# Two AdaLN transformer layers: key and value products over two steps, in-place sums, and reordered heads and FFN ends

## The chip, the cores and the metric

The kernel runs on one core of a Trainium2 chip. The metric is the time of one execution on the device in microseconds (us), as the median of repeated runs; lower is better. A profile of one execution says where that time goes.

## The reference

Two transformer layers with adaptive layer norms on x of 4 x 512 x 512 (float32). Each layer computes six modulation rows per batch from a condition vector, then an attention block and an FFN block, each on a modulated layer norm of x and added back through a gate. The change lies in layer 1 alone, which is:

```python
h = layernorm(x) * (1 + ca) + sa
q = (h @ w_q).reshape(B, S, 8, 4, 128)     # 8 kv heads, 4 query heads each
k = (h @ w_k).reshape(B, S, 8, 128)
v = (h @ w_v).reshape(B, S, 8, 128)
scores = einsum('bqhgd,bkhd->bhgqk', q, k) * 128 ** -0.5, causal
attn = einsum('bhgqk,bkhd->bqhgd', softmax(scores), v)
x = x + ga * (attn.reshape(B, S, 4096) @ w_o)
h = layernorm(x) * (1 + cb) + sb
gate, up = h @ (gate_wq * gate_scale).T, h @ (up_wq * up_scale).T   # 1792 wide, int weights
x = x + gb * ((silu(gate) * up) @ (down_wq * down_scale).T)
```

Layer 0 (a small attention inside each token and an FFN with cluster masks) is untouched.

## The kernel before

**Order.** Until the FFN of layer 1 every engine runs its instructions in the order in which the program text issues them: layer 0 follows a list of step names, layer 1's attention the loop described here. Only layer 1's FFN is left to the scheduler of the framework. Transfers are issued by SP, one queue, in program order; an issue that has to wait holds up those behind it.

**Products in seven.** Each projection of layer 1 (q, k, v and the output o) is a 2 x 2 block product by seven smaller products with sums of blocks ahead of and behind it. `seven` makes seven *pieces*, each a group of matmuls into one PSUM bank and a call of `take`, which adds the bank into the result. Sums of the weights' blocks (`left_sums`, `right_sums`, by `sums_in` and `sums_wo`) run on POOL, in place in the weights' tile (tags wq, wk, wv, wo, one buffer each) and in a second tile (sq, sk, sv, so). For q, k and v, `gather` keeps running sums in two spare tiles `u` and writes the four quarters of the result. For o, seven running sums over the heads stand in `osum`.

**Heads and windows.** 4 batches x 8 kv heads make 32 heads n. A head has 4 query heads s, hence two pairs, and each pair is one step of the pipeline, `window(w)`: window 2n is the first of head n, window 2n+1 the second. Window w computes the scores of pair w+1 (8 tiles: 2 query heads x 4 row blocks of 512, 384, 256 and 128 columns) and the products with V of pair w. In between it runs a list of pieces, the *fill*, spread over 9 slots in order:

```python
share = [len(fill) // slots + (i < len(fill) % slots) for i in range(slots)]
```

In slot i the order is: `flip` of tile i-2 (a 32 x 32 block transpose on DVE), `divide` of tile i-1, `score` of tile i, the product with V (`value`) if i is 6 or 8 (the default of `values`), then that slot's fill. At the window's end `late` issues a load of weights, and `carry(w+1)` issues 16 transfers of 128 KB (SBUF to SBUF) that finish the transpose of the next pair's probabilities into one buffer, `turned`, which `value` reads. The flip of the last tile stands in DVE's order behind the evacuation of the fill of the last slot.

**What fills the windows.** Window 2n holds the seven q pieces of head n+1, and the seven k pieces (n odd, for heads n+1 and n+2) or v pieces (n even, for heads n and n+1). The order is `k[:5] + q[:5] + q[5:] + k[5:]` for odd n; for even n two v pieces alternate with one q piece, and q's last pieces come last. Its `late` is the load of q's weights for head n+2 (1 MB). Window 2n+1 holds the seven o pieces of head n-1, once per batch also four `turn_pieces` that transpose the next batch's norm; its `late` is the load of o's weights for head n (1 MB). The k or v load (0.5 MB) comes behind that window's `carry`. The list order of products is (1, 6, 2, 5, 3, 7, 4) for q, k and v, and (1, 2, 4, 7, 5, 6, 3) for o. Products 4 of q and 3 of o read a block of the loaded weights' tile itself, so the next load into it waits for them.

**The FFN** of layer 1 (`ffn_exact`): for each batch b and each of 14 blocks n of 128 hidden rows, `hidden` computes gate and up, the sigmoid and the two halves of the activation, and `down` adds the product of the block before into four PSUM banks; `leave` multiplies by the gate on DVE, adds to x on POOL and stores. `load` fetches int weights that POOL casts. `leave_attention` ends the attention's sums of batch 3 there.

Of the kernel before, what the change touches and what calls it, by code (L numbers as in the profile page):

```python
# [33 lines left out]
def adaln_two_layers(ctx: ExitStack, tc: tile.TileContext, a, out: bass.AP):  # L34
# [201 lines left out]
    def right_sums(engs, t, s, T1=None):  # L236

        B11, B12, B21, B22 = quarters(t)
        T3, T2, T4 = s[:, 0], s[:, 1], s[:, 2]
        T1 = B12 if T1 is None else T1  # L240
        engs[0].tensor_tensor(T3, B22, B12, SUB)
        engs[1].tensor_tensor(T1, B12, B11, SUB)
        engs[1].tensor_tensor(T2, B22, T1, SUB)  # L243
        engs[1].tensor_tensor(T4, T2, B21, SUB)
        return {1: B11, 2: B21, 3: B22, 4: T4, 5: T1, 6: T2, 7: T3}
# [8 lines left out]
    def sums_wo(n, place="o"):  # L254
        s = T["wp"].tile([P, 3, 2, HALF], F32, tag=f"s{place}", name="so")
        right["o", n] = right_sums((nc.gpsimd, nc.gpsimd), weights["o", n], s)

    def q3(ap):
# [463 lines left out]
    def bank(shape, name):  # L722
        return ps_sc.tile(shape, F32, tag="sc", name=name)
# [27 lines left out]
    def sums_h(b, engs):  # L751
        s = hp.tile([P, 4, 2, HALF], F32, tag="hT", name="hsum")
        right["h", b] = right_sums(engs, h1[b], s, s[:, 3])

# [4 lines left out]
    def gather(start, scale=None):  # L759

        u, c = {}, {}

        def plus(out, v, ps, sign=1):
            if scale is None:
                nc.vector.tensor_tensor(out, v, ps, ADD if sign > 0 else SUB)  # L765
            else:
                nc.vector.scalar_tensor_tensor(out, ps, sign * scale, v, ALU.mult, ADD)

        def take(i, ps):
            if i == 1:  # L770
                c[11], c[12], c[21], c[22] = start()
                size = ps.shape[1] * ps.shape[2]
                for j in (1, 2):
                    t = at.tile([P, size], F32, tag=f"u{j}_{size}", name=f"u{j}", bufs=1)
                    u[j] = t.rearrange("p (m n) -> p m n", m=ps.shape[1])
                if scale is None:
                    nc.scalar.copy(u[1], ps)
                else:
                    nc.scalar.mul(u[1], ps, scale)
            elif i == 6:  # L780
                plus(u[2], u[1], ps)
            elif i == 2:
                plus(c[11], u[1], ps)
            elif i == 5:
                plus(u[1], u[2], ps)
            elif i == 7:
                plus(c[22], u[1], ps)
                plus(u[2], u[2], ps)
            elif i == 3:
                plus(c[12], u[1], ps)  # L790
            else:
                plus(c[21], u[2], ps, -1)

        return take
# [23 lines left out]
    def v_pieces(m):  # L818

        def start():  # L820
            for n in (2 * m, 2 * m + 1):
                vs[n] = at.tile([P, NT, D1], F32, tag="v", name="v")
            v0, v1 = vs[2 * m], vs[2 * m + 1]
            return v0[:, :2], v0[:, 2:], v1[:, :2], v1[:, 2:]

        return seven(lambda: right["h", 2 * m // HKV], lambda: left["v", m], gather(start), SEVENTH)

    def o_pieces(n):
        def take(i, ps):
            if n % HKV == 0:  # L830
                nc.vector.tensor_copy(osum[:, i - 1], ps)
            else:
                nc.vector.tensor_tensor(osum[:, i - 1], osum[:, i - 1], ps, ADD)  # L833

        return seven(lambda: left["o", n], lambda: right["o", n], take, (1, 2, 4, 7, 5, 6, 3))

# [147 lines left out]
    def norm_pieces(xb):  # L984
# [24 lines left out]

        side = [lambda t=t: stats(t) for t in range(NT)]  # L1010
        return out_, side + [ve, nm] + [lambda t=t: xn(t) for t in range(NT)]

# [25 lines left out]
    def gates(pool):  # L1038

        dsb = pool.tile([P, E], F32, name="dsb")  # L1040
        nc.sync.dma_start(dsb, a["L1_ffn_down_scale"].partition_broadcast(P))
        for b in range(B):
            gb[b] = spread(1, 1, b, pool, f"gb{b}")
            nc.gpsimd.tensor_tensor(gb[b], gb[b], dsb, ALU.mult)
# [4 lines left out]
    def decide():  # L1049
        size = small.tile([P, 1], F32, tag="size", name="size", bufs=1)  # L1050
        nc.vector.tensor_reduce(size, sizes, AX.X, ALU.max)
        nc.vector.tensor_scalar(size, size, EXACT, None, ALU.is_gt)
        wide_ps = bank([P, 512], "wide_ps")
        nc.tensor.matmul(wide_ps[:1, :1], size, ones[:, 0:1], start=True, stop=True)
        nc.vector.tensor_copy(wide_i, wide_ps[:1, :1])
# [4 lines left out]
    def split_pieces(got):  # L1060

        def piece(c):
# [3 lines left out]
            for t in range(NT):  # L1066
                nc.tensor.transpose(
                    pt[:, t * P : (t + 1) * P], got["xn"][:, t, c * P : (c + 1) * P], ident
                )
            tm = at.tile([P, E], F32, tag=f"u{1 + c % 2}_{E}", name="tm", bufs=1)  # L1070
            nc.scalar.activation(
# [79 lines left out]
    load("v", 1)  # L1151
    pending = [("v", 1)]

    for n in range(NBLK):
# [5 lines left out]

        k = k_pieces(n // 2 + 1) if n % 2 and ahead else []
        v = v_pieces(n // 2) if n % 2 == 0 and n > 0 else []
        side, turns_ = [[], []], []
# [15 lines left out]
        if 0 < n <= len(pieces):  # L1179
            found = scan(n - 1)  # L1180
            side[1] += [lambda j=j: look(n - 1, j, found[j]) for j in range(2)]
        elif n == len(pieces) + 1:
            side[1].append(decide)
        elif n == len(pieces) + 2:
            side[1].append(small_loads)
        elif n == len(pieces) + 3:
            wide = nc.values_load(wide_i[0:1, 0:1], min_val=0, max_val=P)
        if n == 0:
            window(0, q[:5], values=(8, 9))
        elif ahead:  # L1190
            late = [lambda: load("q", n + 2)] if n + 2 < NBLK else []
            if n == 1:
                fill = q
            elif k:
                fill = k[:5] + q[:5] + q[5:] + k[5:]
            else:
                fill = [f for i in range(3) for f in (v[2 * i], v[2 * i + 1], q[i])] + v[6:] + q[3:]
            window(2 * n, fill, side[0], late)
        else:
            first_weights()  # L1200
            t = split_pieces(got)
            window(2 * n, o[:2] + t[:2] + o[2:3] + t[2:] + o[3:])

            last = o_pieces(n)
# [12 lines left out]
        if 0 < n < NBLK - 2:  # L1217
            sums_in("q", n + 2)
        while pending:
            sums_in(*pending.pop())  # L1220
        if n == 0:
            window(1, q[5:] + k_pieces(1), (), [lambda: load("q", 2)], (8, 9))
            sums_in("q", 2)
        else:
            window(2 * n + 1, o + turns_, side[1], [lambda: load("o", n)])
        sums_o(n)
        m = n // 2 + 2 if n else 2
        if (n % 2 and n > 1 or n == 0) and 2 * m < NBLK:
            load("k", m)
            pending.append(("k", m))  # L1230
        if n % 2 == 0 and n > 0 and n + 2 < NBLK:
            load("v", n // 2 + 1)
            pending.append(("v", n // 2 + 1))
        if behind:
# [4 lines left out]

    for b in (3, 1, 2, 0):  # L1240
        run(*get(b, x[b]))
# [5 lines left out]
    def ffn_exact():  # L1247
        with (
# [39 lines left out]
            def hidden(b, n):  # L1288
# [15 lines left out]
                nc.vector.scalar_tensor_tensor(sg, ps["up"], us, sg, ALU.mult, ALU.mult)  # L1304
                hi = fa.tile([P, S], F32R, tag="act_hi", name="act_hi")
                lo = fa.tile([P, S], F32R, tag="act_lo", name="act_lo")
                halves(hi, lo, sg)
                return hi, lo

            def down(b, n, act, acc):  # L1310
                f, c = divmod(n, NC_)
                w = gu0["down"] if b == f == 0 else gu["down", f]
                for t in range(NT):
                    for i in range(2):
# [4 lines left out]

            def leave(b, acc):  # L1320
                for t in range(NT):
                    tm = temp()
                    nc.vector.tensor_tensor(tm, acc[t], gb[b], ALU.mult)
                    nc.gpsimd.tensor_tensor(x[b][:, t, :], x[b][:, t, :], tm, ALU.add)
                    nc.sync.dma_start(out[b, t * P : (t + 1) * P, :], x[b][:, t, :])

            load(1)
            gates(fx)
            behind, rest = None, sum(leave_attention(B - 1, nc.vector, fx, "ga3", x[B - 1]), [])
            for b in range(B):  # L1330
                acc = [ps_acc.tile([P, 512], F32, tag="acc", name="acc") for t in range(NT)]
                for n in range(NI):
                    if b == 0 and n % NC_ == 0 and n // NC_ + 2 <= NB:
                        load((n // NC_ + 2) % NB)
                    act = hidden(b, n)
                    if behind is not None:
                        down(*behind)
                        if behind[1] == NI - 1:
                            leave(behind[0], behind[3])
                    behind = (b, n, act, acc)  # L1340
                    for _ in range(2):
                        if n > 0 and rest:
                            rest.pop(0)()
                    if n == (8 if b == 0 else 3) and b + 1 < B:
                        split_T(b + 1, normalized(b + 1, xn_place))
            down(*behind)
            leave(behind[0], behind[3])


# [88 lines left out]
```

## Time and profile before

| | us |
|---|---|
| median of 3 runs | 2109.91 (2109.38 to 2116.54) |
| profiled execution, its own time | 2109.82 |
| its span, first to last instruction | 2107.9 |
| PE busy | 2037.2 (97%) |
| DVE / ACT / POOL busy | 1360.0 / 873.5 / 748.6 |
| windows of layer 1's attention | from 211.6 to about 1766 |
| FFN of layer 1 | from 1780.7 to the end |

The page gives busy times per engine and the costliest groups of instructions; the list of waits says which engine waited for which releaser; the timeline of an engine gives each instruction's start and duration, and in square brackets the idle time before it. PE is TensorE, PEld its weight load, DVE VectorE, ACT ScalarE, POOL GpSimd, SPq the queue of SyncE that issues transfers. A float32 matmul stands in the trace as two instructions, and the printed durations of PE overlap: the distance between starts is what one costs.

### The profile page before, as it was taken

Reading aid. Unit: us, or ns where it says so; the run is one execution under the profiler, and the core shown is the slowest. Engines: PE = TensorE matmul, PEld = TensorE weight load, DVE = VectorE, ACT = ScalarE, POOL = GpSimd, SP = SyncE. Lnnn points to the kernel's source line nnn. Section 1 sums busy time; section 2 is a strip of 40 time slices with the busy share of each in tenths; the row PEclk is TensorE's granted clock in tenths of the full one; section 3 lists DMA queues with packets and bytes.
Section 4 is the critical chain, followed back from the end, with each engine's and each line's share of the span. In section 5 each row is a group of like instructions: output and inputs, shape, how many; then the busy total and the mean of one; then the engine's idle time right before and its main releaser. Section 6 shows DMA issues by size and latency. Waiting matters only on the chain.

```text
span 2107.9 us, 27434 instructions
## 1 busy us (share of the span) xinstructions
PE 2037.2 (97%) x9219; PEld 1582.1 (75%) x9219; DVE 1360.0 (65%) x3326; ACT 873.5 (41%) x1997; POOL 748.6 (36%) x653
## 2 busy tenths in 40 slices
PE   6999899999999999999999999999999998999998
PEld 4655677878787777778777777787777876788886
DVE  6766766666667666766676676666665665754543
ACT  3421544444444444544444444444444443332221
POOL 3315243334336343344463334436333422610010
PEclk8799999999999999999999999999999999999999
DMA  8311665665557666556665564656556555500000
GB/s 297 115 60 40 180 160 144 162 164 140 149 147 186 168 157 159 161 137 161 173 181 155 140 178 122 158 143 173 142 148 155 146 121 197 173 21 0 21 21 22
DMA packets 243624, 288.59 MB, mean 137 GB/s; under 512 B 23234, under 2 KB 184002, under 8 KB 243476
## 3 DMA queue, kind: packets, MB, share of 16 engines
q1 hardware_dynamic: 242948, 285.71, 50.1%
q8 instruction: 76, 1.25, 0.2%
q10 hardware_dynamic: 528, 1.05, 0.2%
q14 instruction: 72, 0.59, 0.1%
HBM read 142.99 MB, written 11.57 MB: 73 GB/s over the span
## 4 chain that ended last, share of the span: by engine, by line
PE 80%; DMA 7%; SPq 5%; DVE 3%; issue 2%; POOL 2%; ACT 1%; POOLq 0%; ACTq 0%; DVEq 0%
PE quarter L733 37%; PE av L917 13%; PE sc L868 9%; PE acc L1315 5%; SPq L908 5%; PE p_up L1296 4%; PE p_gate L1296 4%; DMA x<-x 4%; DMA wq<-in_L_attn_w_q_dram 2%; PE ffn L621 2%; PE lnT L464 1%; PE modps L377 1%; PE lg L580 1%; PE qkv_ps L494 1%; PE modT_ps L390 1%
## 5 line engine op out<-in xcount | busy, mean ns | idle before, releaser
L868 PE MATMUL sc<-kT,qT 128*128 128x512 f32 (+3 forms) x1024 | 359.9, 434 | 0.0
L917 PE MATMUL av<-x,v 128*128 128x512 f32 x1008 | 299.6, 441 | 28.9 <-DMA x<-x 13.9
L917 PEld LDWEIGHTS av<-x,v 128*128 128x128 f32 x1008 | 190.2, 193 | 143.4 <-issue 87.4
L883 ACT ACTIVATE x<-x,rden 128x512 f32<-128x512 f32 (+3 forms) x256 | 143.8, 562 | 359.6 <-DVE rden L882 359.5
L871 DVE TENSOR_REDUCE nmx<-sc 128x1 f32<-128x512 f32 (+3 forms) x512 | 251.3, 491 | 17.7
L883 ACT ACTIVATE p<-p,rden 128x512 f32<-128x512 f32 (+3 forms) x256 | 143.8, 562 | 263.8 <-DVE rden L882 263.8
L833 DVE TENSOR_TENSOR acc<-acc,quarter 128x512 f32<-128x512 f32 x196 | 134.4, 686 | 160.1 <-PE quarter L733 158.1
L230 POOL TENSOR_TENSOR sq<-wq 128x512 f32<-128x512 f32 x32 | 40.7, 1272 | 536.0 <-DMA wq<-in_L_attn_w_q_dram 464.5
L868 PEld LDWEIGHTS sc<-kT,qT 128*128 128x128 f32 x1024 | 186.3, 191 | 21.0
L733 PEld LDWEIGHTS quarter<-wo,oT 128*128 128x128 f32 x768 | 146.5, 191 | 54.5 <-issue 24.1
L733 PE MATMUL quarter<-wo,oT 128*128 128x256 f32 x768 | 183.1, 382 | 2.8 <-DMA wo<-in_L_attn_w_o_dram 2.2
L873 ACT ACTIVATE p<-sc,nmx 128x512 f32<-128x512 f32 (+3 forms) x256 | 135.1, 528 | 111.4 <-DVE nmx L871 103.3
L765 DVE TENSOR_TENSOR qT<-u,quarter 128x512 f32<-128x512 f32 x128 | 87.9, 687 | 135.9 <-PE quarter L733 135.8
L869 DVE TENSOR_TENSOR sc<-sc,mask 128x128 f32<-128x128 f32 x512 | 144.8, 283 | 25.0 <-PE sc L868 23.9
L873 ACT ACTIVATE x<-sc,nmx 128x512 f32<-128x512 f32 (+3 forms) x256 | 135.0, 527 | 55.0 <-DVE nmx L871 46.8
L886 DVE STREAM_TRANSPOSE p<-p 128x512 f32<-128x512 f32 (+3 forms) x256 | 129.4, 506 | 20.1 <-ACT p L883 18.7
L886 DVE STREAM_TRANSPOSE x<-x 128x512 f32<-128x512 f32 x248 | 125.1, 504 | 2.1 <-ACT x L883 1.2
L765 DVE TENSOR_TENSOR u<-u,quarter 128x256 f32<-128x256 f32 (+1 forms) x144 | 85.4, 594 | 63.3 <-PE quarter L733 46.6
L733 PE MATMUL quarter<-hsum,sq 128*128 128x256 f32 x512 | 121.1, 379 | 1.4 <-DVE hsum L243 1.4
L733 PE MATMUL quarter<-hT,wq 128*128 128x256 f32 x512 | 121.6, 380 | 0.1
L733 PE MATMUL quarter<-hsum,wq 128*128 128x256 f32 x512 | 121.0, 379 | 0.0
L733 PE MATMUL quarter<-so,soT 128*128 128x256 f32 x512 | 121.0, 379 | 0.0
(249 smaller groups left out, 3765.8 us busy)
## 6 DMA issues: line engine op xcount, KB each, us to landing
x<-p SPq DMA_DIRECT2D x512, 128.0 KB, 2.7
x<-x SPq DMA_DIRECT2D x496, 128.0 KB, 2.9
wq<-in_L_attn_w_q_dram SPq DMA_DIRECT2D x32, 1024.0 KB, 5.2
wo<-in_L_attn_w_o_dram SPq DMA_DIRECT2D x32, 1024.0 KB, 5.3
wm<-in_L_wmod_dram SPq DMA_DIRECT2D x12, 1024.0 KB, 9.8
wk<-in_L_attn_w_k_dram SPq DMA_DIRECT2D x16, 512.0 KB, 3.6
wv<-in_L_attn_w_v_dram SPq DMA_DIRECT2D x16, 512.0 KB, 3.7
xn<-x_d SPq DMA_DIRECT2D x28, 256.0 KB, 4.2
```

Of the source, the lines that this page charges most:

```text
L733: nc.tensor.matmul(ps[:, m, :], l[:, k, m * P : (m + 1) * P], r[:, k, :], start=(k == 0), stop=(k == 1),)
L765: nc.vector.tensor_tensor(out, v, ps, ADD if sign > 0 else SUB)
L833: nc.vector.tensor_tensor(osum[:, i - 1], osum[:, i - 1], ps, ADD)
L868: nc.tensor.matmul(ps[:, :w], q[:, i * P : w], kT[n][:, :w], start=True, stop=True)
L869: nc.vector.tensor_tensor(ps[:, i * P : w], ps[:, i * P : w], mask, ADD)
L871: nc.vector.tensor_reduce(nmx, ps[:, :w], AX.X, ALU.max, negate=True)
L873: nc.scalar.activation(blocks(s, i), ps[:, :w].rearrange("p (j q) -> p j q", q=BK), AF.Exp, bias=nmx, accum_out=den,)
L883: nc.scalar.mul(p, p, rden)
L886: nc.vector.transpose(blocks(s, i), blocks(s, i))
L908: nc.sync.dma_start(dst, src[:, j])
L917: nc.tensor.matmul(av.rearrange("p (a n) -> p a n", a=NG)[:, :, BK * k :], vs[n][:, k, :], pT[:, k, :, P * (s % 2) + BK * k : P * (s % 2 + ...
L1296: nc.tensor.matmul(ps[kind], w[kind][:, k, c * P : (c + 1) * P], h2[b % 2][i][:, k, :], start=(k == 0 and i == 0), stop=(k == KC - 1 and i ...
```

## The change

- **Key and value products over two steps.** Their seven pieces are cut: three run in the second window of the head before, behind o's third piece; the other four in the next first window, in twos around q's first two. The loads of k and v are issued at the end of first windows, and their sums on POOL at the end of second ones. V gets 4 buffers.
- **Sums in place.** `gather` keeps its running sums in the result's quarters; the tiles `u` are gone.
- **First heads.** Window 0 takes six q pieces instead of five; three v pieces run in window 1; window 2 has its value products in slots 7 and 9.
- **Last heads.** Output weights of head 30 come in two halves through the k and v tiles, the order of its products is (1, 2, 3, 7, 5, 6, 4), and a small sigmoid runs on ACT ahead of the last products. Head 31's temporaries use the tiles of V and K.
- **Other.** `decide` is split into two parts in two windows; the pieces of the norm have gaps between their last entries; x is read back in another order.
- **FFN's ends.** The sums of `leave_attention` run on POOL instead of DVE, `dsb` and `ga` share one tile, the last three `down` steps of batch 3 run tile by tile, and the last `leave` adds on DVE.

```diff
     def gather(start, scale=None):
-        u, c = {}, {}
+        c = {}
...
             if i == 1:
                 c[11], c[12], c[21], c[22] = start()
...
-                    nc.scalar.copy(u[1], ps)
+                    nc.scalar.copy(c[11], ps)
...
             elif i == 6:
-                plus(u[2], u[1], ps)
+                plus(21, 11, ps)
             elif i == 2:
-                plus(c[11], u[1], ps)
+                plus(11, 11, ps)
             elif i == 5:
-                plus(u[1], u[2], ps)
+                plus(22, 21, ps)
+            elif i == 3:
+                plus(12, 22, ps)
             elif i == 7:
-                plus(c[22], u[1], ps)
-                plus(u[2], u[2], ps)
-            elif i == 3:
-                plus(c[12], u[1], ps)
+                plus(22, 22, ps)
+                plus(21, 21, ps)
             else:
-                plus(c[21], u[2], ps, -1)
+                plus(21, 21, ps, -1)
...
+    def load_half(n, i):
+        w = T["wp"].tile([P, 2, GW], F32, tag=f"w{'kv'[i]}", name="wo_half")
+        g = n % HKV
+        rows = slice(g * GW + i * GW // 2, g * GW + (i + 1) * GW // 2)
+        nc.sync.dma_start(w, a["L1_attn_w_o"][rows, :].rearrange("(k p) n -> p k n", p=P))
+        weights["o", n] = weights.get(("o", n), ()) + (w[:, :, :HALF], w[:, :, HALF:])
...
         if n == 0:
-            window(0, q[:5], values=(8, 9))
+            window(0, q[:6], values=(8, 9))
         elif ahead:
             late = [lambda: load("q", n + 2)] if n + 2 < NBLK else []
             if n == 1:
-                fill = q
-            elif k:
-                fill = k[:5] + q[:5] + q[5:] + k[5:]
+                window(2, q, side[0], late, (7, 9))
             else:
-                fill = [f for i in range(3) for f in (v[2 * i], v[2 * i + 1], q[i])] + v[6:] + q[3:]
-            window(2 * n, fill, side[0], late)
+                window(2 * n, begun[:2] + q[:2] + begun[2:] + q[2:], side[0], late)
+                begun = []
+                if 2 * (m + 1) < NBLK:
+                    load(kind, m + 1)
+                    pending.append((kind, m + 1))
+                else:
+                    load_half(NBLK - 2, 1 - n % 2)
         else:
             first_weights()
             t = split_pieces(got)
             window(2 * n, o[:2] + t[:2] + o[2:3] + t[2:] + o[3:])
+            warm = small.tile([P, 1], F32, tag="warm", name="warm", bufs=1)
+            nc.scalar.activation(warm, ones[:, 0:1], AF.Sigmoid)
...
-        while pending:
-            sums_in(*pending.pop())
         if n == 0:
-            window(1, q[5:] + k_pieces(1), (), [lambda: load("q", 2)], (8, 9))
+            sums_in("v", 1)
+            begun = v_pieces(1)
+            window(1, q[6:] + k_pieces(1) + begun[:3], (), [lambda: load("q", 2)], (8, 9))
+            begun = begun[3:]
             sums_in("q", 2)
+            load("k", 2)
+            pending.append(("k", 2))
         else:
-            window(2 * n + 1, o + turns_, side[1], [lambda: load("o", n)])
+            if n > 1 and n + 2 < NBLK:
+                begun = (v_pieces if n % 2 else k_pieces)(n // 2 + 1)
+            now, begun = begun[: min(n + 1, 3)], begun[min(n + 1, 3) :]
+            late = [lambda: load("o", n)] if n + 2 < NBLK else []
+            window(2 * n + 1, o[:3] + now + o[3:] + turns_, side[1], late)
+            while pending:
+                sums_in(*pending.pop())
         sums_o(n)
-        m = n // 2 + 2 if n else 2
-        if (n % 2 and n > 1 or n == 0) and 2 * m < NBLK:
-            load("k", m)
-            pending.append(("k", m))
-        if n % 2 == 0 and n > 0 and n + 2 < NBLK:
-            load("v", n // 2 + 1)
-            pending.append(("v", n // 2 + 1))
...
-    for b in (3, 1, 2, 0):
+    for b in (3, 0, 2, 1):
         run(*get(b, x[b]))
...
-            def leave(b, acc):
-                for t in range(NT):
+            def leave(b, acc, tiles=range(NT), eng=nc.gpsimd):
+                for t in tiles:
                     tm = temp()
                     nc.vector.tensor_tensor(tm, acc[t], gb[b], ALU.mult)
-                    nc.gpsimd.tensor_tensor(x[b][:, t, :], x[b][:, t, :], tm, ALU.add)
+                    eng.tensor_tensor(x[b][:, t, :], x[b][:, t, :], tm, ALU.add)
...
-            behind, rest = None, sum(leave_attention(B - 1, nc.vector, fx, "ga3", x[B - 1]), [])
+            behind, rest = [], sum(leave_attention(B - 1, nc.gpsimd, fx, "ga3", x[B - 1]), [])
...
-                    if behind is not None:
-                        down(*behind)
-                        if behind[1] == NI - 1:
-                            leave(behind[0], behind[3])
-                    behind = (b, n, act, acc)
+                    if behind and (b + 1 < B or n < NI - 2):
+                        done = behind.pop()
+                        down(*done)
+                        if done[1] == NI - 1:
+                            leave(done[0], done[3])
+                    behind.append((b, n, act, acc))
...
-            down(*behind)
-            leave(behind[0], behind[3])
+            for t in range(NT):
+                for step in behind:
+                    down(*step, (t,))
+                leave(B - 1, acc, (t,), nc.vector)
```

## The prediction

> **What bounds the kernel now.** I read the page first, then the list of waits on PE, then the timelines of PE and SP over the steps of layer 1's attention.
>
> ```profile
> PE 2037.2 (97%) x9219; PEld 1582.1 (75%) x9219; DVE 1360.0 (65%) x3326; ACT 873.5 (41%) x1997; POOL 748.6 (36%) x653
> ```
>
> PE is the bound, and the change removes no matmul from it. It can only win or lose idle PE time. The list of waits (engine, line, releaser: total us, times, longest) says where the idle time in the attention is:
>
> ```profile
> PE av L917 <- DMA x<-x: 13.9, 10, 2.1
> PE av L917 <- DMA xn<-x_d: 5.5, 3, 2.0
> PE av L917 <- DMA x<-p: 4.8, 1, 4.8
> PE av L917 <- issue: 1.7, 1, 1.7
> PE av L917 <- DMA x_d<-xn: 1.6, 2, 0.9
> ```
>
> All five are the first product with V of a window (`value`, L917), waiting for `carry` (L908), the 16 transfers that turn the probabilities. Without window 0's 4.8 they make 22.7 us, 23 below. Two windows, in the PE and SP timelines (start, duration, engine, line, tiles, count), show when this wait arises:
>
> ```profile
> 580.59 1.02 PE L868 MATMUL sc<-kT,qT 128*128 128x512 f32 x2
> ...
> 595.04 2.32 PE L917 MATMUL av<-x,v 128*128 128x512 f32 x8
> ...
> 628.28 1.02 PE L868 MATMUL sc<-kT,qT 128*128 128x512 f32 x2
> ...
> 644.53 2.39 PE L917 MATMUL av<-x,v 128*128 128x512 f32 x8 [1.64 <-DMA x<-x]
> ```
>
> ```profile
> 576.71 0.37 SPq L208 DMA_DIRECT2D wq<-in_L_attn_w_q_dram  x1
> 581.49 10.29 SPq L908 DMA_DIRECT2D x<-x  x16
> ...
> 628.51 0.37 SPq L208 DMA_DIRECT2D wq<-in_L_attn_w_q_dram  x1
> 629.42 11.29 SPq L908 DMA_DIRECT2D x<-x  x16
> ```
>
> Both are second windows of a head (2n+1), and in both the `carry` starts about 1 us after the window's first score. In the first, the 1 MB load of q weights was issued 3.9 us ahead of the window. The value product starts 14.45 us into it, with no wait. In the second, q's last piece ran in the last slot of the window before. The load waits for that piece (it frees the weights' buffer), is issued at +0.23, and shares the DMA engines with the `carry`. The issues then take 11.3 us, not 10.3, and the value product starts at +16.25. I call this a *late load*. Over the fourteen windows of the second kind (after every even head) that start lies between 15.4 and 16.7, mean 16.1.
>
> **What the Trainium skill says.** "DMA: Bandwidth & Descriptors", Queues, rings and completion order: one queue's transfers run on its rings of the same 16 engines, whose descriptors are consumed in ring order. So a 1 MB load issued just ahead of a 2 MB `carry` is served first; the 1.6 us above agree. "TensorE: Matmul & The Clock Gate", Part 1: PE's clock is halved after an idle window of a free-running 3.4 us. The trace agrees, but the threshold is lower than a wholly idle window: a wait of 1.95 us is enough when it falls inside one such window.
>
> ```profile
> 1620.20:1623.60 3.40, 1.45 (x5) 0.68 (x4) 1.86 (x5) 1.18 (x3) 0.66 (x1) 1.00 0.92 292
> 1623.60:1627.00 3.40, 3.40 (x10) 2.52 (x9) 0.00 (x0) 0.59 (x1) 0.00 (x0) 0.50 0.05 17
> ```
>
> (After the stretch's length come the busy us of PE, PEld, DVE, ACT, POOL, then the granted clock.) 57% idle, then 3.4 us at half clock, which loses 1.7 us. The wait of 2.12 us at 742 was cut in two by the boundary and cost nothing more. "ScalarE: Activation LUTs", What ACT_TABLE_LOAD costs: 1.28 us for the load; the trace has 1.28 at 1782.9.
>
> **The change, part by part.** Prices, from PE starts: a q or o piece 1.73 us, k .86, v .89; scores ahead of the slot-6 value product (tiles 0 to 6) 4.1.
>
> *In-place sums.* Eight vector results and one copy per seven products, before and after. Nothing is saved or added; DVE at 65% hides either order.
>
> *Spread of k and v.* Three of the seven pieces move to the window before, behind o's third. PE's sum is unchanged. What counts is the time from a window's start to its first value product (slot 6, behind the fill of slots 0 to 5), and which piece ends the window:
> - First windows (2n) hold 11 pieces in 9 slots: 2, 2, then 1 each. Before the value product: 4 k/v and 4 q = 3.5 + 6.9, with scores 14.5 us. Before the change it was 17.3 (v) or 18.8 (k), so no wait.
> - Second windows hold 10 pieces: 2, then 1 each. Before the value product: 4 o and 3 k/v = 6.9 + 2.6, with scores 13.6 us. Before the change it was 14.45.
> - q's last piece is now in slot 8 of every first window, so every q load is late. o's seventh piece moves from slot 6 (its load was issued 2.2 us before the window ended) to slot 8, so every o load is late too. Both last products (4 of q, 3 of o) read the loaded tile itself.
>
> The flip of the last tile stands behind the last piece's evacuation on DVE (628.48 + .69, flip to 629.39), so the `carry` again starts at +1.14. I take 16.1 for the arrival in both kinds of window. Waits: 16.1 - 13.6 = 2.5 in second windows, 16.1 - 14.5 = 1.6 in first ones. Windows with `turn_pieces` (heads 5, 13, 21) are long and end with transposes, and neither they nor the windows after them wait. That leaves 25 second windows (heads 2 to 29) x 2.5 = 62 and 25 first windows (heads 3 to 30) x 1.6 = 40. Window 3 (no late load, arrival about 14.1, product at 12.8) gives 1.3, window 4 (9 pieces, product at 12.8) 3.3, and the three windows whose `carry` starts at +1.88 another 2. Sum 109, less the 23 that go: **+86**.
>
> Both ends for the arrival: below, 14.2 (start 1.14, issues 10.3, 1.9 to the last packet and .85 to PE's start, as in undisturbed windows), which leaves .6 x 25 = 15 us in all; above, 16.7, which adds 30.
>
> *Half clock.* A wait of 2.5 us puts over 1.9 us into one 3.41 us window in some 60% of positions (a 2.1 us stretch of 3.41). 25 x .6 x 1.7 = 25, less one such stretch that goes: **+24**; bounds 0 and 45. Waits of 1.6 stay under the threshold.
>
> *Moved loads and sums.* The k or v load (0.5 MB, one issue of .4 to .6) moves on SP from behind the first windows' `carry` to behind the second windows'. It waits for pieces four slots earlier, so it holds nothing up; at worst its packets touch the end of that `carry` (0 to .5 each, in the upper bound). Its four POOL sums (.73 each, 2.9 us) now stand ahead of o's eight (1.27 each), which are wanted a window later, 24 us on. POOL is at 36%: nothing.
>
> *First heads.* One more q piece in window 0 runs inside its 4.85 us wait: -1.7, and one half-clock stretch of two goes: -1.7. `decide` in two parts: -1.2 (PE waits 1.17 at 1317.9). *Last heads.* Output weights of head 30 come in halves, two and one windows ahead; that takes away 2.23 at 1729.3 and its half clock, less about .3 for the copy of the last values: -3.7. *FFN's start.* The sigmoid's table is loaded ahead (-1.3), and seven sums of .69 go from DVE to POOL, where they take 1.27 each, 9 us. Against that, `ga` now waits for `dsb`'s tile until POOL's products end at 1795, with weight loads behind it on SP. I take -4, bounds -8 and +4. *Without a price:* x's reload in another order (16 transfers issued from 1754.9 to 1767.9, under the last head's work; uncovered, one landing of 5.3 us), the temporaries of head 31 in V's and K's tiles (free by then) and a third buffer for the FFN's activations. *Tail.* The last three down products run tile by tile and DVE adds (.69) instead of POOL (4 x 1.27 in a row). PE ends .9 later, the last store is issued 2.1 sooner: **-2**. These parts: **-14**, bounds -22 to -4.
>
> **Sum:** 86 + 24 - 14 = +96 on the profiled execution's own 2109.82 (its span 2107.9), which equals the median of the runs, 2109.91. So **2206 us**.
>
> **Rivals.**
> 1. *The wait goes, the loads do not hurt.* If the late loads don't delay the `carry` (arrival 14.2), first windows don't wait and second ones wait .6: 15 + 1 + 1 - 23 - 14 = -20, **2090**, faster. For it: a window's sum of work falls from 26.9 and 20.7 to 24.1 and 23.3, which is what an evening-out should do. Against it: fourteen of fourteen late loads in the trace came at 15.4 or later. It decides from an arrival below about 14.8, where waits equal what is saved.
> 2. *Half way.* The arrival falls to 15.2, for instance because the steadier steps leave less of the scans' and other transfers' traffic in that stretch: 25 x 1.6 + 25 x .7 + 6 - 23 - 14 = +26, no half clock: **2136**.
> 3. *The FFN's start lags.* POOL's 9 us of sums delay the weights' casts and PE waits some 8 us there; on top of the likeliest case 2214, on rival 1 2098. It changes no sign by itself.
>
> **How the numbers follow.** Likeliest case 75%, its own range 2162 to 2238 (arrival 15.7 to 16.5, half clock 0 to 45, ends -22 to -4); half way 9%; rival 1 16%, nearly all of it faster. About 0.5%, 10.5 us, is what a measurement of this kernel can tell from no change; 4% lie within it, between rivals 1 and 2. Faster .16, same .04, slower .80. The range 2112 to 2232 leaves out rival 1 and the top of the likeliest case.
>
> **What would show it.** In the changed kernel's profile: PE's wait at the value product in nearly all windows, about 2.5 us in second and 1.6 in first ones, some 110 us in all under DMA; windows of 25.8 us each; every weight load of q and o issued within .3 us after a window's start and the `carry` at +1.1; a dozen or more half-clock stretches. It is wrong if the `carry` lands before +14.5 despite a late load, or if the last piece of a window no longer gates the load.

## The result, and the profile after

| | before | after |
|---|---|---|
| median, us | 2109.77 (4 runs) | 2221.41 (4 runs, 2213.98 to 2221.98) |
| ratio | | **1.0513**, 95% interval 1.0483 to 1.0544 |
| span of the profiled execution | 2107.9 | 2219.7 |
| PE idle at the first value product, windows 1 to 61 | 22.8 | 110.0 |
| half-clock time, windows 1 to 61 | 1 stretch | 16 stretches of 3.41 us |

The changed kernel is 5% slower. The forecast was 2206 us. On the page after, PE does the same 9219 matmuls; its busy time is 26 us longer because more of it runs at half clock.

```profile
PE 2063.6 (93%) x9219; PEld 1590.9 (72%) x9219; DVE 1356.3 (61%) x3323; ACT 876.4 (39%) x1998; POOL 754.9 (34%) x656
```

The list of PE's waits after (engine, line, releaser: total us, times, longest):

```profile
PE av L927 <- DMA x<-x: 30.8, 13, 3.2
PE av L927 <- DMA x<-p: 22.3, 14, 3.4
PE av L927 <- DMA wv<-in_L_attn_w_v_dram: 15.9, 5, 3.7
PE av L927 <- DMA wk<-in_L_attn_w_k_dram: 15.5, 5, 3.3
...
PE av L927 <- DMA scan<-in_L_ffn_gate_wqT_dram: 7.3, 3, 4.0
PE av L927 <- DMA scan<-in_L_ffn_up_wqT_dram: 6.8, 4, 2.0
PE p_up L1322 <- DVE tm L1329: 5.2, 1, 5.2
```

The six `av` lines are one wait: the first value product of a window (L927 now), waiting for the `carry` (L918). Before, it stood in sixteen windows with at most 2.1 us (window 0 apart). The releaser named is whatever DMA landed last; `value` reads nothing of `wk` or of a scan, and all these waits stand at the same instruction of their windows. The last line is new, at the FFN's start.

The timelines of PE and SP show a second window (scores start at 601.45) and the first window after it (629.86):

```profile
601.45 1.02 PE L878 MATMUL sc<-kT,qT 128*128 128x512 f32 x2
...
618.38 1.95 PE L927 MATMUL av<-x,v 128*128 128x512 f32 x3 [3.09 <-DMA wk<-in_L_attn_w_k_dram]
...
629.86 1.02 PE L878 MATMUL sc<-kT,qT 128*128 128x512 f32 x2
...
646.02 2.17 PE L927 MATMUL av<-x,v 128*128 128x512 f32 x6 [1.43 <-DMA scan<-in_L_ffn_up_wqT_dram]
```

```profile
601.68 0.37 SPq L208 DMA_DIRECT2D wq<-in_L_attn_w_q_dram  x1
602.59 11.73 SPq L918 DMA_DIRECT2D x<-x  x16
...
630.09 0.37 SPq L208 DMA_DIRECT2D wo<-in_L_attn_w_o_dram  x1
631.00 11.03 SPq L918 DMA_DIRECT2D x<-p  x16
```

In both, the weights' load is issued at +0.23 and the `carry` at +1.14. PE is ready at +13.8 and +14.7 (the run-up: from a window's first score to where only the `carry` is missing) and starts at +16.9 and +16.2 (the arrival at PE). The stretches around the first of these waits (after the length: busy us of PE, PEld, DVE, ACT, POOL, then the granted clock):

```profile
614.97:618.38 3.41, 0.32 (x2) 0.03 (x1) 2.59 (x7) 2.55 (x6) 0.00 (x0) 1.00 0.85 219
618.38:621.80 3.42, 3.42 (x7) 2.00 (x8) 0.00 (x0) 0.00 (x0) 2.36 (x4) 0.61 0.00 1
```

A stretch with PE mostly idle is followed by one at 0.61, the mean of full clock up to 619.13 and half clock from there: a half-clock stretch of 3.41 us, which loses 1.7 us more after the wait of 3.1.

By stages, from PE starts in the two traces: window 0 and what is ahead of it -4.0, windows 1 to 61 **+116.0**, window 62 and the last head -3.7, FFN's start **+6.5** (from its first gate product to that of the sixth hidden block, 32.2 to 38.7), the rest -3.1. Together +111.7, the difference of the spans.

### The profile page after: what moved, and what is told of

Read it like the earlier page. It is cut to its first block, busy times and chain, and to the rows that moved or that the text cites. A ratio compares the mean times of both kernels' runs of the same rounds, so it can differ in the third digit from the quotient of the medians.

```text
span 2219.7 us, 27450 instructions
## 1 busy us (share of the span) xinstructions
PE 2063.6 (93%) x9219; PEld 1590.9 (72%) x9219; DVE 1356.3 (61%) x3323; ACT 876.4 (39%) x1998; POOL 754.9 (34%) x656
## 4 chain that ended last, share of the span: by engine, by line
PE 56%; DMA 23%; SPq 12%; DVE 5%; issue 2%; POOL 1%; ACT 1%; DVEq 0%; ACTq 0%; POOLq 0%
PE quarter L746 19%; PE av L927 14%; SPq L918 12%; DMA x<-p 8%; DMA x<-x 6%; PE acc L1341 4%; PE p_gate L1322 4%; PE p_up L1322 4%; DMA wq<-in_L_attn_w_q_dram 3%; PE sc L878 2%; PE ffn L634 2%; DMA wo<-in_L_attn_w_o_dram 2%; DMA wk<-in_L_attn_w_k_dram 1%; DMA wv<-in_L_attn_w_v_dram 1%; PE lnT L477 1%
## 5 line engine op out<-in xcount | busy, mean ns | idle before, releaser
L927 PE MATMUL av<-x,v 128*128 128x512 f32 x1008 | 323.5, 467 | 115.1 <-DMA x<-x 30.8
L927 PEld LDWEIGHTS av<-x,v 128*128 128x128 f32 x1008 | 199.1, 203 | 252.6 <-issue 167.1
L778 DVE TENSOR_TENSOR qT<-qT,quarter 128x512 f32<-128x512 f32 x224 | 150.7, 684 | 239.2 <-PE quarter L746 236.6
L746 PE MATMUL quarter<-wo,oT 128*128 128x256 f32 x744 | 173.6, 382 | 0.6 <-ACT p L909 0.4
L746 PEld LDWEIGHTS quarter<-wo,oT 128*128 128x128 f32 x744 | 141.1, 193 | 33.1 <-issue 7.9
L932 ACT COPY oT<-av 128x512 f32<-128x512 f32 x128 | 74.7, 584 | 151.5 <-PE av L927 150.2
L746 PEld LDWEIGHTS quarter<-hT,wq 128*128 128x128 f32 x512 | 97.2, 190 | 32.4 <-issue 14.8
```

What stands on the lines that cost most here:

```text
L746: nc.tensor.matmul(ps[:, m, :], l[:, k, m * P : (m + 1) * P], r[:, k, :], start=(k == 0), stop=(k == 1),)
L778: nc.vector.tensor_tensor(c[out], c[v], ps, ADD if sign > 0 else SUB)
L927: nc.tensor.matmul(av.rearrange("p (a n) -> p a n", a=NG)[:, :, BK * k :], vs[n][:, k, :], pT[:, k, :, P * (s % 2) + BK * k : P * (s % 2 + ...
```

## The experiments

Theory 1 is the prediction's: the late load delays the `carry`, PE gets to its first value product sooner, and the wait is the arrival less the run-up. Theory 2: only the shorter run-up counts. Theory 3: the moved k and v pieces themselves cost the time. Unless said otherwise, each edit is to the changed kernel. The table gives the ratio to the kernel before, run beside it on the same chip.

| | edit | us | ratio, 95% interval | wait at first value product |
|---|---|---|---|---|
| 1 | load behind the carry | 2196.0 | 1.0409 (1.0387 to 1.0431) | 17.3 |
| 2 | values in slots 7, 9 | 2081.3 | 0.9866 (0.9850 to 0.9883) | 0 |
| 3 | o ahead of k/v | 2085.7 | 0.9893 (0.9875 to 0.9911) | 7.2 |
| 4 | before, o load late | 2139.3 | 1.0134 (1.0114 to 1.0154) | 24.4 |
| 5 | values in slots 6, 9 | 2084.2 | 0.9886 (0.9870 to 0.9903) | 6.2 |
| 6 | values in slots 7, 8 | 2127.0 | 1.0100 (1.0081 to 1.0118) | 19.0 |
| 7 | before, values 7, 9 | 2108.3 | 0.9999 (0.9990 to 1.0009) | 0.2 |
| 8 | late loads from ACT's queue | 2249.5 | 1.0681 (1.0663 to 1.0698) | 113.4 |
| 9 | before, values 6, 9 | 2078.0 | 0.9848 (0.9826 to 0.9871) | 2.8 |
| 10 | 2, and sums on DVE | 2077.8 | 0.9843 (0.9819 to 0.9866) | 0 |
| 11 | 10, and own `dsb` | 2074.4 | 0.9832 (0.9813 to 0.9851) | 0 |

**1. The load behind the carry.**

```diff
-        run(*late)
         if w + 1 < LAST:
             carry(w + 1)
+        run(*late)
```

> The changed kernel with one edit: at a window's end the late 1 MB load of q or o weights is issued behind the 16 transfers of `carry`, not ahead of them. Theory 1 (the load delays the carry): the carry lands at about +14.2 in every window. First windows (run-up 14.7) then wait 0, second ones (run-up 13.8) 0.4 x 25 = 10 us, window 4 about 1.4; of 110 us some 14 are left, and the 16 half-clock stretches (26 us) go: about 2100 us. Theory 2 (the carry is bound by its own 16 issues, and the shorter run-up alone makes the wait): arrival and waits stay, about 2220. Theory 3 (the moved k and v pieces themselves cost the time): also about 2220.

The arrival did what theory 1 says. The last packet of a `carry` came at +13.3 in first windows (15.5 after the change) and +13.8 in second ones, and the wait fell from 110.0 to 17.3 us. In one second window, from 608.11 on, SP and PE show:

```profile
609.28 10.30 SPq L918 DMA_DIRECT2D x<-x  x16
619.70 0.53 SPq L208 DMA_DIRECT2D wq<-in_L_attn_w_q_dram  x1
622.26 2.39 PE L927 MATMUL av<-x,v 128*128 128x512 f32 x8 [0.31 <-issue]
```

The issues take 10.3 us again, not 11.7, and the value product starts at +14.15. Theory 2 falls, and so does theory 3 for these waits: the moved pieces stand where they stood. But the total fell by 25 us only, not by 120. Eight waits of 7.3 to 15.2 us each, 74.4 in all, had come in their place, with longer half-clock stretches around them. POOL's, DVE's and PE's timelines show one of them:

```profile
492.54 1.26 POOL L242 TENSOR_TENSOR so<-wo 128x512 f32<-128x512 f32 x1 [11.19 <-DMA wo<-in_L_attn_w_o_dram]
...
497.78 1.02 POOL L1012 TENSOR_TENSOR rstd<-ve,mhalf 128x4 f32<-128x4 f32 x1
```

```profile
498.83 0.16 DVE L1016 SCALAR_TENSOR_TENSOR nmr<-bnmv,rstd 128x4 f32<-128x4 f32 x1 [13.26 <-POOL rstd L1012]
```

```profile
500.53 2.05 PE L746 MATMUL quarter<-hT,sq 128*128 128x256 f32 x4 [9.37 <-DVE kT L780]
```

The `wo` load is issued some 12 us later in this window, POOL stands 11.19 us in front of its sums, the norm's small `rstd` is queued behind them, DVE stands 13.26 us in front of `nmr`, and PE finds k not evacuated. My expectation priced the load's landing at nothing; it had left out who waits for the load. Of the other seven waits, three stand at k or v in the same way, three at ACT's copy of a value product, and one, the longest, at the `wq` load itself; they were not followed further.

**2. Value products in slots 7 and 9.**

```diff
-    def window(w, fill, side=(), late=(), values=(6, 8)):
+    def window(w, fill, side=(), late=(), values=(7, 9)):
```

> The changed kernel with one edit: a window's two value products stand in slots 7 and 9, not 6 and 8, so one piece more runs ahead of the first. The loads stay late. Theory 1 (wait = arrival less run-up): arrival stays at about 16.5 and 16.2; run-up becomes 15.8 in second and 16.7 in first windows; waits 0.7 x 25 = 17 us in second, 0 in first, some 20 in all, and most half-clock stretches go: about 2105 us. Theory 2 says the same. Theory 3 (the moved pieces themselves cost the time): unchanged, about 2220.

All waits at the first value product in windows 1 to 61 are gone, more than was expected (of other waits of PE 4.3 us are there, 1.0 after the change). With the moved pieces still in place, theory 3 falls here for the total too. And the arrival did not stay: the last packets came at +13.0 and +12.7. The edit does two things. Besides the longer run-up, the second value product (2.2 us) now stands behind the window's last piece. SP issued the load 1.9 us before the window's end and the `carry` at +0.19. Experiments 5 and 6 take the two apart.

**3. o ahead of k and v.**

```diff
-            window(2 * n + 1, o[:3] + now + o[3:] + turns_, side[1], late)
+            window(2 * n + 1, o + now + turns_, side[1], late)
```

> The changed kernel with one edit: in second windows all seven pieces of o run ahead of the three of k or v. Then o's last piece stands in slot 5, its load is issued some 10 us ahead of the next window, and seven o pieces (12.1 us) with 4.1 of scores make a run-up of 16.3. Theory 1: first windows lose the late load, land at 14.2 against a run-up of 14.7 and wait 0; second windows keep the late q load, land at 16.5 and wait about 0.2 x 25 = 5; with window 4 under 10 us in all, no half clock: about 2095 us. Theory 2 (loads do not matter): second windows 0.2 x 25 = 5, first windows keep their 1.5 x 25 = 38: about 2130. Theory 3: about 2220.

First windows wait 0.3 us in all. Second windows keep the late q load: packets until +15.1, PE's start at +16.5 on average against a run-up of 16.3, 5.2 us in all. Arrival less run-up holds here with both terms measured, and the 2130 of theory 2 is ruled out. The total is 10 us below what I expected. The spans of the two traces differ by 137 us; waits and sixteen half-clock stretches make 130 of it, and the rest was not traced.

**4. The kernel before, with the o load late.**

```diff
-            window(2 * n + 1, o + turns_, side[1], [lambda: load("o", n)])
+            window(2 * n + 1, o[:6] + [lambda: None] * 2 + o[6:] + turns_, side[1], [lambda: load("o", n)])
```

> The kernel before with one edit: two empty entries in second windows put o's last piece into the last slot, so that every o load is late there too; nothing else moves, and the run-up of second windows stays 14.45. Theory 1 (a late load costs only where the run-up is shorter than the arrival): the loads make the carries of first windows arrive at about 16.2, but their run-up is 17.3 or 18.8, so nothing new waits: about 2110 us, same. Rival (a late load costs time wherever it is, by holding up other transfers): 1.5 x 25 = 38 us more, about 2148.

The carries of first windows land 1.9 us later (+15.6, not +13.7) and no first window waits. So a late load with a run-up of 17 to 19 us costs nothing at the value product, as theory 1 says. Yet the total rose by 31 us, and for the most part not for the rival's reason. The moved piece had stood between the two value products; without it they stand back to back:

```profile
598.52 2.32 PE L917 MATMUL av<-x,v 128*128 128x512 f32 x8
600.67 0.39 PE L868 MATMUL sc<-kT,qT 128*128 128x128 f32 x2
601.51 2.42 PE L917 MATMUL av<-x,v 128*128 128x512 f32 x8 [0.45 <-ACT oT L922]
```

The second product waits until ACT has copied the first one out of the PSUM buffer. Such second windows are 21.44 us long, not 20.72. This wait is listed with 15.7 us, 33 times (2.0, three times before). In the last head a wait for `wo` grew from 2.2 to 5.4 us (here the rival is right, for 3 us), and the half-clock time between 243 and 1838 us, which costs half its length, from 17.1 to 23.9 us. My "nothing else moves" was wrong.

**5. Only the second value product moved.**

```diff
-    def window(w, fill, side=(), late=(), values=(6, 8)):
+    def window(w, fill, side=(), late=(), values=(6, 9)):
```

> The changed kernel with one edit: only the second value product of a window moves, from slot 8 to slot 9, behind the last piece; the first stays in slot 6, so the run-up stays 13.8 and 14.7. Theory 1 (what costs is that the last piece ends the window, so that load and carry start only in the next one): with 1.9 us of a value product behind the last piece, the load is issued some 1.9 us before the window ends and the carry at +0.2, as in the kernel with slots 7 and 9; the carry lands at about 12.6, PE could start at 13.5, nothing waits, and the half-clock stretches go: about 2090 us. Rival (the shorter run-up is what costs, wherever the loads stand): waits stay, about 2215 us.

This is the cleanest test, as the run-up is untouched. SP's and PE's timelines at a window's end:

```profile
621.28 0.37 SPq L208 DMA_DIRECT2D wq<-in_L_attn_w_q_dram  x1
623.40 10.59 SPq L918 DMA_DIRECT2D x<-x  x16
```

```profile
621.05 2.32 PE L927 MATMUL av<-x,v 128*128 128x512 f32 x8
623.20 1.02 PE L878 MATMUL sc<-kT,qT 128*128 128x512 f32 x2
...
636.79 2.32 PE L927 MATMUL av<-x,v 128*128 128x512 f32 x8
```

The load goes out at 621.28, 1.9 us ahead of the next window (623.20), and the `carry` at +0.20. The value product starts at +13.59 with no wait; in the same window before the edit it stood until +16.33. Load and `carry` both start earlier here, so this run does not divide the 2.7 us between them; the 0.94 us of the `carry`'s start and the 1.5 to 2.2 us that the load was worth in experiment 1 account for it. The wait fell from 110.0 to 6.2 us and the total by 137. A short run-up alone costs next to nothing.

**6. Only the first value product moved.**

```diff
-    def window(w, fill, side=(), late=(), values=(6, 8)):
+    def window(w, fill, side=(), late=(), values=(7, 8)):
```

> The changed kernel with one edit: only the first value product of a window moves, from slot 6 to slot 7; the last piece still ends the window, so loads stay late and carries stay at +1.14. Theory 1 (wait = arrival less run-up): arrival stays 16.5 and 16.2, run-up becomes 15.7 and 16.4; waits 0.8 x 25 = 20 us in second windows, 0 in first, about 25 in all with windows 3 and 4, and few half-clock stretches are left: about 2112 us. Rival (the run-up has no part, the late start of load and carry delays the whole window): waits stay, about 2215 us.

Loads stayed late and carries at +1.14; the last packets came at +15.4 and +15.2, as after the change. The waits fell to 19.0 us (17.0 of them in second windows) and the half clock to one stretch in windows 1 to 61. Both terms of the difference are thus shown, one at a time. The total is 15 us above what I expected. In ten windows that carry extra work (a batch's norm or the attention's last sums), the second product, with one piece or one small transpose between it and the first, now waits for ACT's copy (1.2 to 3.2 us a time, 16.7 in all).

**7. The kernel before, values in slots 7 and 9.**

```diff
-    def window(w, fill, side=(), late=(), values=(6, 8)):
+    def window(w, fill, side=(), late=(), values=(7, 9)):
```

> The kernel before, with its value products in slots 7 and 9 as in the second experiment. If the spread of k and v gains nothing in itself and only the position of the value products counts, the kernel before also loses its waits (22.8 us) and its half-clock stretch: about 2084 us, within 5 us of the changed kernel with the same edit (2081). If the spread gains something in itself once its waits are gone, this stays some 20 us above it, at about 2100.

The old wait went (0.2 us left), and the total did not move. It had turned into another, as the list of PE's waits and the timeline show:

```profile
PE av L917 <- ACT oT L922: 24.9, 37, 0.8
```

```profile
599.59 2.42 PE L917 MATMUL av<-x,v 128*128 128x512 f32 x8 [0.67 <-ACT oT L922]
```

Seven pieces in nine slots leave slots 7 and 8 of a second window empty, so the products stand back to back again.

**8. The late loads from ACT's queue.**

```diff
-        nc.sync.dma_start(w, src.rearrange("(k p) n -> p k n", p=P))
+        T.get('q', nc.sync).dma_start(w, src.rearrange("(k p) n -> p k n", p=P))
...
+        T['q'] = nc.scalar
         run(*late)
+        T['q'] = nc.sync
```

> The changed kernel with one edit: the late 1 MB loads of q and o weights are issued by ACT's DMA queue, at the same place, while the carry stays on SP's. If the carry is delayed because it stands behind the load in the rings of one queue, it now lands at 14.2 again, the waits fall to some 14 us and the half-clock stretches go: about 2100 us. If it is delayed because both share the 16 DMA engines, arrival and waits stay: about 2215 to 2225 us.

ACT's and SP's timelines, in a window that starts at 651.23:

```profile
651.47 0.38 ACTq L208 DMA_DIRECT2D wo<-in_L_attn_w_o_dram  x1
```

```profile
652.40 11.21 SPq L918 DMA_DIRECT2D x<-p  x16
```

On two queues the `carry` still takes 11.2 us to issue, and its last packets come at +15.6 and +15.1 on average, as from one queue. So it isn't the order within one queue that delays it. What load and `carry` still share are the core's 16 DMA engines: over the 12 us from this `carry`'s first issue to 664.4 their busy share reads 0.94 to 1.13 (the view's figure can exceed 1), and over the 12 us from 581.6 in the kernel before, where the load came early, 0.52 to 0.87. That the sharing makes the delay fits this and the other runs, but no run changed it alone. The kernel was 28 us slower than the change. The waits explain 3.4 of it and the half-clock time (81.9 us between 243 and 1838, not 54.6) some 14; a wait of 6.0 for `wq` is new. What ACT's own issuing adds to the rest was not separated.

**9. The kernel before, values in slots 6 and 9.**

```diff
-    def window(w, fill, side=(), late=(), values=(6, 8)):
+    def window(w, fill, side=(), late=(), values=(6, 9)):
```

> The kernel before, with only its second value product moved, from slot 8 to slot 9. In the seventh experiment the two products stood back to back in second windows (seven pieces in nine slots leave slots 7 and 8 empty), and the second one waited 0.67 to 0.85 us for the first one's PSUM buffer; here o's last piece lies between them. If the spread of k and v gains nothing in itself: loads and carries start earlier, the waits (22.8 us) and the half-clock stretch (1.7) go, no new wait comes: about 2084 us, the same as the changed kernel with this edit (2084). If the spread gains some 25 us in itself: about 2105.

One digit in the kernel before takes its waits from 22.8 to 2.8 us and no back-to-back pair comes: 2078.0. That is 6 us below the changed kernel with the same edit, measured on different chips (ratios 0.9848 and 0.9886). The totals alone do not show what the spread is worth, because the FFN's start is 6.2 us longer in the changed kernel. Windows 1 to 61, where the spread lies, take 1453.0 us here, 1455.2 in experiment 5 and 1449.7 in experiment 2. So with its waits gone, the spread of k and v shows next to no gain, 3.3 us at best.

**10 and 11. The FFN's start**, on the kernel of experiment 2.

```diff
-    behind, rest = [], sum(leave_attention(B - 1, nc.gpsimd, fx, "ga3", x[B - 1]), [])
+    behind, rest = [], sum(leave_attention(B - 1, nc.vector, fx, "ga3", x[B - 1]), [])
```

```diff
-    def gates(pool):
+    def gates(pool, acts=None):
...
-        dsb = pool.tile([P, E], F32, tag="ga3", name="dsb")
+        if acts:
+            dsb = acts.tile([P, E], F32, tag="act_lo", name="dsb", bufs=3)
...
-            gates(fx)
+            gates(fx, fa)
```

> The changed kernel with value products in slots 7 and 9 (2081 us), and besides with the seven sums at the FFN's start on DVE again, as in the kernel before. If these sums on POOL make the first p_up product wait (DVE stands at nmr for the rstd that POOL computes behind them): the wait of 5.2 us falls to about 1.7 as before, and the FFN's start gets 3 to 6 us shorter: about 2077 us. Rival (ga's tile, which now waits for dsb's, is what costs): the start stays, 2081.

> The tenth experiment's kernel, and besides dsb in a free buffer of the FFN's activations, so that ga no longer waits for POOL's products on it. If that wait is what makes act_lo late (PE waits 3.4 us there, 1.4 in the kernel before), another 2 us go: about 2075 us. If it costs nothing, as the tenth experiment: about 2077.

In the changed kernel POOL's timeline has the sums, then the cast, then the norm's `rstd`; DVE and PE stand behind it:

```profile
1893.88 1.27 POOL L976 TENSOR_TENSOR acc<-acc 128x512 f32<-128x512 f32 x1
1895.10 1.04 POOL L1311 CAST gate<-wi 128x1024 fp32r<-128x1024 int32 x1
1896.09 1.02 POOL L68 TENSOR_TENSOR rstd<-ve,mhalf 128x4 f32<-128x4 f32 x1
```

```profile
1897.14 0.98 DVE L70 SCALAR_TENSOR_TENSOR nmr<-bnmv,rstd 128x4 f32<-128x4 f32 x1 [3.70 <-POOL rstd L68]
```

```profile
1899.85 3.35 PE L1322 MATMUL p_up<-h,first 128*128 128x512 f32 x7 [5.17 <-DVE tm L1329]
```

With the sums on DVE the wait at `p_up` is 1.75 again (PE's timeline of experiment 10):

```profile
1764.57 2.11 PE L1322 MATMUL p_up<-h,first 128*128 128x512 f32 x8 [1.75 <-DVE tm L1329]
```

The FFN's start goes from 39.7 (experiment 2) to 36.5 us, and with `dsb` in its own place to 32.2, the length before the change. There `ga` is issued 3.1 us after the first gate product, not 15.2 after it. So the sums on POOL cost 3.2 us and the shared tile 4.3 in these profiles. Part of both is the clock: the stretch has 13.7, 6.8 and 0 us of half clock in the three, and PE's idle time there is 9.5, 8.2 and 5.6 us. These are read from one profile each; the totals (2081.3, 2077.8, 2074.4) go the same way, but neighbouring intervals overlap. Experiment 11 is the fastest version run, 1.7% below the kernel before (1.5 to 1.9 by the interval). Experiment 9, run beside it, is 3.6 us slower, and their intervals overlap: nearly all that was won came with the one digit.

## Why the prediction was right, and where not

| step | predicted | measured |
|---|---|---|
| arrival at PE, second / first windows | 16.1 / 16.1 | 16.5 / 16.2 |
| run-up, second / first | 13.6 / 14.5 | 13.8 / 14.7 |
| waits in 25 second windows | 62 | 67.5 (2.70 each) |
| waits in 25 first windows | 40 | 38.2 (1.53 each) |
| windows 3 / 4 | 1.3 / 3.3 | 0.2 / 4.0 |
| waits less those that go | +86 | +87.2 |
| half clock in windows 1 to 61 | +24 | +25.6 (16 stretches, one before) |
| ahead of window 1 | -3.4 | -4.0 |
| window 62 and the last head | -3.7 | -3.7 |
| FFN's start | -4 (-8 to +4) | **+6.5** |
| rest of the FFN, with the tail | -2 | -3.1 |

- **The main mechanism held.** A late load ahead of every `carry`, and a run-up too short for it. Experiments 1, 5 and 6 show each term by itself: put the load behind the `carry`, start both earlier, or lengthen the run-up, and the wait goes by about that much. Rival 1 (the loads do not hurt) and rival 2 (half way) fall: in none of the 50 windows did PE start before +15.4.
- **The half clock held**, number and size. In experiment 6, with waits of at most 1.6 us for the `carry`, one stretch is left in windows 1 to 61, and that one follows a wait of 3.2 for ACT's copy. The forecast had 15 stretches in second windows and none after waits of 1.6; 14 came there, one in window 4, and one after a wait of 1.98 us in a first window.
- **The gain ahead of window 1 came out by luck.** Experiments 1 to 3, 5, 6, 8, 10 and 11 run the same program up to there and took 244.1 to 255.7 us, the kernel before and experiments 4, 7 and 9 245.4 to 247.6; how much half-clock time falls into this stretch differs from run to run.
- **Window 3 was over-sized.** I took an arrival of 14.1; its `carry` started at +0.19, and PE started at +13.2.
- **The FFN's start failed in sign.** The failed step is the -4 that I took for the table load ahead and the sums moved to POOL. I counted the 9 us of sums on POOL and that the tile would delay `ga`, but I took POOL's time there for free. What stood behind these sums was the next norm's 1 us `rstd`, for which DVE waits, and behind DVE stands PE. Rival 3 had the place, and nearly the size (its +4 against +6.5), but under the weights' casts; experiments 10 and 11 name the sums ahead of `rstd`, and the tile as the larger part.
- **One reason given was not needed, though its number was right.** I explained the delay with the Trainium skill's "DMA: Bandwidth & Descriptors", Queues, rings and completion order: a transfer ahead in the same queue is served first. Experiment 8 put the load on another queue and the delay stayed, so it does not hang on the order within one queue. The page's sentence itself was not tested.
- **The miss of 15 us** is mostly this: 10.5 at the FFN's start and 3 in waits and half clock. Windows 1 to 61 grew by 116.0, of which waits and half clock make 112.8; the remaining 3 were not traced.

## What to carry to other kernels

Before work is evened out over the steps of a pipeline, ask which item ends each step and what it releases: here the last product of a step held a buffer, its load and then the next transfer, and one product moved behind it was worth more than the whole spread. A wait is an arrival less a run-up, so get both from the trace and move one at a time. When a wait goes, look at once for the next in-order queue: POOL's small `rstd` behind large sums, and two products back to back on one PSUM buffer, each ate what an edit had won.

## What the runs showed that was not expected

- A 1 MB load issued 0.9 us ahead of a 2 MB transfer of 16 pieces moves the end of that transfer by 1.5 to 2.2 us, from the same queue or from another one.
- Two value products on one PSUM buffer, with nothing or only a 0.4 us score between them, made their window 0.7 to 0.9 us longer, 33 to 37 times a run (experiments 4 and 7); in experiment 7 that was as much as the edit had taken away.
- All half-clock stretches of the changed kernel begin on one grid of 3.41 us. Cut on this grid, windows 1 to 61 show where the limit lies: PE was idle for 58% to 99% of each of the 15 pieces just ahead of a stretch (909.27 to 912.68: busy 1.43 of 3.41 us), and no piece with 55% or less idle was followed by one (of two with 58%, one was). A wait of 2 us is thus enough, if it falls inside one piece.
